# Moving stores and transposing transfers from the sync queue to GpSimd's queue in a Macaron S4D layer

## The chip, the core and the metric

The kernel runs on one core of one Trainium2 chip. The metric is the device time in microseconds of one execution; the figure for a kernel is the median of several runs. The names in the profile are: PE is TensorE's matmul queue and PEld its weight loads, DVE is VectorE, ACT is ScalarE, POOL is GpSimd, SP is SyncE (which here only issues transfers). A name with a q behind it, such as SPq, is an engine's own instruction queue: the time in which it issues a transfer or waits to do so.

## The reference

A Macaron layer on x of shape 4 x 1024 x 256: half a feed-forward network, then a state-space (S4D) convolution along the sequence, then half of the same feed-forward network again. Each part normalises its input and adds its result to it.

```
x = x + 0.5 * ffn(layernorm(x))
x = x + s4d(layernorm(x))
x = x + 0.5 * ffn(layernorm(x))

def ffn(x):
    h = silu((x @ w1.T) * s1) * ((x @ w2.T) * s2)     # 256 -> 1024
    h = gelu((h @ h1.T) * s3)                          # 1024 -> 1024
    h = gelu((h @ h2.T) * s4)                          # 1024 -> 1024
    return (h @ w3.T) * s5                             # 1024 -> 256

def s4d(x):                    # per channel, along the 1024 positions
    K = 2 * Re(sum_n C_n * exp(dtA_n * t))
    y = irfft(rfft(x, 2048) * rfft(K, 2048))[:1024]
    return gelu(y) @ W.T + b
```

The gelu is the exact one. The weights w1, w2, h1, h2 and w3 are ternary (-1, 0, 1).

## The kernel before

The tokens are cut into 16 feed-forward blocks of 512: eight "f" blocks take x to the intermediate x1, eight "g" blocks take x2 to the output. One batch element is two blocks. Between an f pair and a g pair lies the convolution of that batch element, `mix(b)`, which takes x1 to x2. All intermediates (x1, x2, the spectrum `k_hat`, and a scratch array `moved`) lie in DRAM.

A block's matmuls run in four stages. Layer 1 is 16 groups of four matmuls (`pa`, `pb`). Layers 2 and 3 are eight groups of 16 matmuls each, 128x512 outputs. The output product `po` has 64 matmuls of 128x256. Activations come in two parts, a rounded value and the rest that rounding left (`low_part`, L257), so each weight tile is used with both. ScalarE does the activation and the rounding, VectorE the rest. After `po`, VectorE scales the result (L375), GpSimd adds the residual `xr` (L383) and the sum is stored (L384).

The convolution is work for every engine, in small steps, and these steps are woven into the feed-forward blocks. `tick()` is called after each output of layers 2 and 3 (15 times a block) and advances the generator `aside` by one step: first the convolution's kernel (`pk`, L595 to L625), then its spectrum (matrices `m_k`, results stored in `k_hat`), then the four mixes. A mix loads half a batch element (`xm`, L173), normalises it, multiplies it by the transform's matrices (`m_m`, loaded at L653, product `pf_m` at L664), multiplies by the spectrum (L759 to L761), transforms back (`pi`, matrices `mi`), and applies W (`pw`), whose result `yw` gets its residual on GpSimd (L868) and is stored (L869).

From the fifth block on, every third tick also advances `weight_checks`: 44 steps, each of which loads a piece of a weight (`given`, L418) and counts where it differs from its rounded copy. At the end the counts are reduced (`total`, L433), a matmul adds the partitions (`p_bad`, L435) and the result goes to `bad`. After the layer a register loads `bad`; if it isn't 0, the layer is run again at full precision.

`ahead()` is called after each output of layer 3 and advances `prepare` for the next block: load its x (`load_x`, L188, four transfers of 128 KB), normalise (L234 to L244), and `squares` (L276). The latter is a transpose by way of DRAM: VectorE transposes 32x32 squares (`sq`, L282), eight transfers of 64 KB put them at their places in `moved` (L286), two transfers of 256 KB bring `moved` back as `xf` (L292). When layer 3 is through, `parted` (L301, L257) makes the two parts `xt` that the next block's layer 1 reads.

Before the change all of these transfers after the start are issued by SP, in one order. The program is written in one order of statements; a list scheduler of the framework reorders within each engine, with its own estimates of times, and places the waits. Each engine runs its instructions in order, so an instruction that waits holds those behind it. What lies behind what on SP is set by this order. Three pools matter: the tag `xb` (x, xm, x_g before normalisation) has three buffers, `half` has 19[...].

In the first block GpSimd issues the weight loads and the first x loads.

Of the kernel before, what the change touches and what calls it, by code (L numbers as in the profile page):

```python
# [94 lines left out]
def macaron_layers(  # L95
# [23 lines left out]
    nc = tc.nc  # L119
# [39 lines left out]
    x2 = dram.tile([B, L, D], F32, name="x2")  # L159

    moved = dram.tile([DC, P, JT, P], F32, name="moved")
    k_hat = dram.tile([2 + len(PAIRS), 2, P, 2, D], F32, name="k_hat")
# [4 lines left out]
    def positions(t, b, j, n=2):  # L167
        return t[b].rearrange("(p j) d -> p j d", j=J)[:, j : j + n, :]
# [8 lines left out]
    def tokens(t, blk, a=0, n=JT):  # L177
        b, g = divmod(blk, J // JT)
        rows_of = t[b, g * TB : (g + 1) * TB, :]
        return rows_of.rearrange("(q a) d -> q a d", a=JT)[:, a : a + n, :]  # L180
# [11 lines left out]
        return w.rearrange("(k p) o -> p k o", p=P)  # L192


    weights_from = nc.gpsimd if split else nc.sync

    x_first = work.tile([P, JT, D], F32, tag="xb", name="x_f0", bufs=3)
# [78 lines left out]
    def squares(xn, name):  # L276


        out = []
        for k in range(DC):  # L280
            sq = half(f"sq_{name}_{k}", P // SQ, JT, SQ)
            nc.vector.transpose(  # L282
                sq, xn[:, :, k * P : (k + 1) * P].rearrange("p j (c r) -> p c j r", r=SQ)
            )
            for a in range(JT):
                nc.sync.dma_start(  # L286
                    moved[k].rearrange("(c r) a q -> a r c q", r=SQ)[a],
                    sq[a * SQ : (a + 1) * SQ].rearrange("r c j s -> r c (j s)"),
                )
        for k in range(DC):  # L290
            t = half(f"xf_{name}_{k}")
            nc.sync.dma_start(t, moved[k].rearrange("d a q -> d (a q)"))  # L292
            out.append(t)
        return out

# [23 lines left out]
    def ffn(xt, src, dst, blk, name, tick, ahead, final):  # L319

        ha = []
        for m in range(KH):
            pa, pb = bank(f"pa_{name}_{m}"), bank(f"pb_{name}_{m}")
            linear(pa, w1_sb, m, xt)
            linear(pb, w2_sb, m, xt)
            g = half(f"g_{name}_{m}")
            t = ring(f"ha_{name}_{m}", parts, TB, dtype=wide)
            nc.scalar.activation(g, pa, AF.Silu, scale=sc_sb[:, 0, m : m + 1])  # L330
            stt(g if split else t[:, 0, :], pb, sc_sb[:, 1, m : m + 1], g, ALU.mult, ALU.mult)
            if split:
                nc.scalar.copy(t[:, 0, :], g)  # L333
                low_part(t, g)
            ha.append(t)
        for layer, w in ((2, h1_sb), (3, h2_sb)):
            hb = []
            for m in range(KH):
                ps = bank(f"p{layer}_{name}_{m}")
                linear(ps, w, m, ha)  # L340
                t = ring(f"h{layer}_{name}_{m}", parts, TB, dtype=wide)
                g = half(f"g{layer}_{name}_{m}") if split else t[:, 0, :]
                nc.scalar.activation(g, ps, AF.Gelu, scale=sc_sb[:, layer, m : m + 1])  # L343
                if split:
                    nc.scalar.copy(t[:, 0, :], g)  # L345
                    low_part(t, g)
                hb.append(t)
                if layer == 3:
                    ahead()
                if m < KH - 1:  # L350
                    tick()
            ha = hb
        ahead(last=True)
        tick()
        rest = []
        for i in range(0, JT, 2):
            xr = half(f"xr_{name}_{i}", 2, D)
            nc.sync.dma_start(xr, tokens(src, blk, i, 2))
            rest.append(xr)

        def result(ps, i, n):

            for e in range(n):
                for k in range(KH):
                    for part in range(parts):
                        nc.tensor.matmul(  # L366
                            ps[:, e * D : (e + 1) * D],
                            ha[k][:, part, (i + e) * P : (i + e + 1) * P],
                            w3_sb[:, k, :],
                            start=(k == 0 and part == 0),  # L370
                            stop=(k == KH - 1 and part == parts - 1),
                        )

        def finish(ps, y, xr, i, n, add_on):
            stt(  # L375
                y,
                ps.rearrange("p (e d) -> p e d", e=n),
                0.5,
                w3s_sb[:, None, :].to_broadcast([P, n, D]),
                ALU.mult,  # L380
                ALU.mult,
            )
            add_on.tensor_tensor(y, xr, y, ALU.add)  # L383
            nc.sync.dma_start(tokens(dst, blk, i, n), y)  # L384

        for i in range(0, JT, 2):
            y = half(f"y_{name}_{i}", 2, D)
            if final and i + 2 == JT:
                for e in range(2):
                    ps = bank(f"po_{name}_{i + e}")  # L390
                    result(ps, i + e, 1)
                    finish(
                        ps[:, 0:D],
                        y[:, e : e + 1, :],
                        rest[i // 2][:, e : e + 1, :],
                        i + e,
                        1,
                        nc.vector,
                    )
            else:  # L400
                ps = bank(f"po_{name}_{i}")
                result(ps, i, 2)
                finish(ps, y, rest[i // 2], i, 2, nc.gpsimd)

    def weight_checks():

        todo = []
        for src, held in ((w1, w1_sb), (w2, w2_sb), (h1, h1_sb), (h2, h2_sb), (w3, w3_sb)):
            n_k, width = held.shape[1], held.shape[2]
            by = max(1, 512 // width)  # L410
            for k in range(0, n_k, by):
                for c in range(0, width, 512):
                    cols = slice(c, min(c + 512, width))
                    todo.append((rows(src)[:, k : k + by, cols], held[:, k : k + by, cols]))
        assert len(todo) == N_CHECKS
        for n, (src, held) in enumerate(todo):
            given = half(f"given_{n}", *held.shape[1:])
            nc.sync.dma_start(given, src)  # L418
            stt(
                given,  # L420
                given,
                0.0,
                held.bitcast(F32),
                ALU.add,
                ALU.not_equal,
                accum_out=miss[:, n : n + 1],
            )
            yield

        total = small.tile([P, 1], F32, name="total")  # L430
        ones = small.tile([P, 1], F32, name="ones")
        nc.vector.memset(ones, 1.0)
        nc.vector.tensor_reduce(total, miss[:, 0:N_CHECKS], axis=mybir.AxisListType.X, op=ALU.add)  # L433
        ps = psum.tile([1, 1], F32, tag="ps", name="p_bad")
        nc.tensor.matmul(ps, total, ones, start=True, stop=True)  # L435
        nc.vector.tensor_copy(bad, ps)
# [276 lines left out]
    def kernel_spectrum():  # L713

        def rows_of(j):
            return taps[j // 2][:, j % 2].rearrange("p h d -> p (h d)")

        got = None
        for got in spectrum(rows_of, "k", over=NB // J):
            yield  # L720
        minus = half("k_minus", 2, D)
        for n, m in enumerate((0, 4)):
            t = got[m]
            nc.scalar.mul(minus[:, n, :], t[:, 1, :], -1.0)
            for e in range(2):
                nc.sync.dma_start(k_hat[n, 0, :, e], t[:, 0, :])
            nc.sync.dma_start(k_hat[n, 1, :, 0], minus[:, n, :])
            nc.sync.dma_start(k_hat[n, 1, :, 1], t[:, 1, :])
            yield
        for n, (a, b) in enumerate(PAIRS):  # L730
            n += 2
            minus = half(f"k_minus_{n}", 2, D)
            t, o = got[a, b], got[b, a]
            nc.scalar.mul(minus[:, 0, :], o[:, 1, :], -1.0)
            nc.sync.dma_start(k_hat[n, 0, :, 0], t[:, 0, :])
            nc.sync.dma_start(k_hat[n, 0, :, 1], o[:, 0, :])
            nc.sync.dma_start(k_hat[n, 1, :, 0], minus[:, 0, :])
            nc.sync.dma_start(k_hat[n, 1, :, 1], t[:, 1, :])
            yield

    def mix(b):
# [23 lines left out]
        r, i = factors(0)  # L765
# [6 lines left out]
        for n, (p, q) in enumerate(PAIRS):  # L772
            r, i = following
# [72 lines left out]
        for j in range(0, J, 2):  # L846
# [19 lines left out]
                ALU.add,  # L866
            )
            nc.gpsimd.tensor_tensor(y, xr, y, ALU.add)  # L868
            nc.sync.dma_start(positions(x2, b, j), y)  # L869
        yield  # L870


# [147 lines left out]
```

## Time and profile before

| | us |
|---|---|
| median of 3 runs | 1464.32 (1463.37 to 1466.54) |
| the profiled execution | 1462.53 |
| its span, first to last instruction | 1460.8 |
| DVE busy | 839.0 (57%) |
| ACT busy | 682.4 (47%) |
| mean granted TensorE clock | 0.987 of full |

Device time of the profiled execution is 1.7 us above its span; the profile's rows refer to the span.

The queues, from the page: transfers, MB, and the share that their packets took of the 16 DMA engines' time.

```profile
q1 hardware_dynamic: 64800, 85.79, 18.7%
q0 software_dynamic: 5168, 13.96, 2.9%
```

The hardware queue carries what SP and ScalarE issue, the software queue what GpSimd issues. The longest stays of SP's queue before an instruction (total us, times, longest us):

```profile
SPq L286 <- DVE sq_f L282: 229.2, 7, 69.8
SPq L384 <- POOL y_g L383: 146.0, 15, 62.9
SPq L286 <- DVE sq_g L282: 129.9, 8, 57.5
SPq L384 <- POOL y_f L383: 93.4, 16, 17.1
SPq L869 <- POOL yw L868: 76.9, 16, 16.1
```

Most of this is time in which SP has nothing else that it could usefully do; the row alone doesn't tell how much. Times from issue to landing of the transfers that the change concerns, and of loads behind them (medians, us): moved 1.7, xf 2.8 (g) and 3.4 (f), stores of y 2.0, stores of yw 3.0, k_hat 1.7 to 1.8; m_m 4.5, m_k 4.3, xm 4.1, x_g 3.3. Of transfers that GpSimd issues: x_f 7.5, w_sb 4.3 (256 KB) to 21.1 (1 MB), all in the start, where 361 GB/s are moved in the first fortieth of the span against a mean of 69.

Reading the timeline: start, duration, engine, line, operation, output and inputs, how many, and in brackets how long the engine had been idle and what ended it. Durations of an SPq row are those of issuing, not of the transfer. For the DMA rows of POOL the same holds.

### The profile page before, as it was taken

To read this page: it belongs to the slowest core of one execution; us is meant where nothing else is said; L and a number is where in the kernel's file an instruction comes from. 1 tells how busy PE (TensorE), PEld (TensorE's weight loads), DVE (VectorE), ACT (ScalarE), POOL (GpSimd) and SP (SyncE) were. 2 spreads that over 40 slices of the span, in tenths; PEclk is the share of its full clock that TensorE was granted. 3 is DMA by queue.
4 is the path that set the end of the run, shared out by engine and by line. 5 is a ranking of instruction groups with operands and counts; after the bars stand their busy time and mean duration, and the time that the engine had idled before them with its cause. 6 is when DMAs were issued, how large, how long until landed. Compare 5 with 4: busy or idle time off the path is not lost.

```text
span 1460.8 us, 18295 instructions
## 1 busy us (share of the span) xinstructions
PE 1418.2 (97%) x6972; PEld 1197.8 (82%) x6972; DVE 839.0 (57%) x1614; ACT 682.4 (47%) x1037; POOL 87.6 (6%) x91
## 2 busy tenths in 40 slices
PE   9999999998999999999999998999979989999997
PEld 7878888887888888888788887888868878888886
DVE  6886657743735687453877534857436757351421
ACT  5875468644435444343353433534245334353442
POOL 4010000100000000010000010000000000100000
PEclk9999999999999999999999999999989999999999
DMA  9120201102123140240332123231240320210200
GB/s 361 40 71 0 59 15 35 39 8 80 55 76 101 44 159 17 85 130 15 109 94 72 59 79 102 67 99 45 71 145 16 94 65 32 93 49 1 65 8 18
DMA packets 70210, 101.27 MB, mean 69 GB/s; under 512 B 7952, under 2 KB 34832, under 8 KB 70112
## 3 DMA queue, kind: packets, MB, share of 16 engines
q1 hardware_dynamic: 64800, 85.79, 18.7%
q0 software_dynamic: 5168, 13.96, 2.9%
q8 instruction: 56, 0.92, 0.3%
q14 instruction: 42, 0.34, 0.1%
q10 hardware_dynamic: 144, 0.26, 0.1%
HBM read 76.91 MB, written 23.07 MB: 68 GB/s over the span
## 4 chain that ended last, share of the span: by engine, by line
PE 89%; DVE 3%; DMA 3%; ACT 2%; SPq 1%; issue 1%; POOL 0%; DVEq 0%; POOLq 0%
PE p_g L311 30%; PE p_f L311 27%; PE po_g L366 4%; PE pa_f L311 4%; PE pa_g L311 4%; PE pb_f L311 4%; PE pb_g L311 4%; PE po_f L366 3%; PE pf_m L664 2%; PE pi L834 2%; PE pw L854 2%; PE pk L595 1%; SPq L286 1%; DMA m_m<-in_cosm_dram 1%; PE pf_k L664 0%
## 5 line engine op out<-in xcount | busy, mean ns | idle before, releaser
L311 PE MATMUL p_f<-h_f,h_sb 128*128 128x512 f32 x1024 | 239.3, 392 | 0.0
L311 PE MATMUL p_g<-h_g,h_sb 128*128 128x512 f32 x1024 | 238.4, 393 | 0.0
L311 PE MATMUL p_f<-ha_f,h_sb 128*128 128x512 f32 x1024 | 237.2, 391 | 0.0
L311 PE MATMUL p_g<-ha_g,h_sb 128*128 128x512 f32 x1024 | 235.0, 390 | 0.0
L311 PEld LDWEIGHTS p_g<-h_g,h_sb 128*128 128x128 f32 x1024 | 194.0, 189 | 40.7
L311 PEld LDWEIGHTS p_g<-ha_g,h_sb 128*128 128x128 f32 x1024 | 192.1, 188 | 39.7
L311 PEld LDWEIGHTS p_f<-h_f,h_sb 128*128 128x128 f32 x1024 | 191.8, 188 | 39.9
L311 PEld LDWEIGHTS p_f<-ha_f,h_sb 128*128 128x128 f32 x1024 | 191.6, 188 | 40.1 <-ACT ha_f L333 0.2
L257 DVE TENSOR_TENSOR h_g<-g_g,h_g 128x512 fp32r<-128x512 f32 x128 | 88.2, 690 | 230.4 <-ACT h_g L345 230.4
L343 ACT ACTIVATE g_g<-p_g,sc_sb 128x512 f32<-128x512 f32 x128 | 88.3, 690 | 282.2 <-PE p_g L311 274.4
L257 DVE TENSOR_TENSOR h_f<-g_f,h_f 128x512 fp32r<-128x512 f32 x128 | 87.8, 690 | 189.7 <-ACT h_f L345 189.3
L343 ACT ACTIVATE g_f<-p_f,sc_sb 128x512 f32<-128x512 f32 x128 | 88.1, 689 | 216.6 <-PE p_f L311 198.4
L345 ACT CAST h_g<-g_g 128x512 fp32r<-128x512 f32 x128 | 79.1, 620 | 3.7
L345 ACT CAST h_f<-g_f 128x512 fp32r<-128x512 f32 x128 | 78.5, 618 | 2.9
L330 ACT ACTIVATE g_g<-pa_g,sc_sb 128x512 f32<-128x512 f32 x64 | 43.7, 689 | 76.7 <-PE pa_g L311 73.4
L311 PE MATMUL pa_g<-xt_g,w_sb 128*128 128x512 f32 x256 | 69.8, 391 | 2.6 <-DVE xt_g L301 2.6
L311 PE MATMUL pa_f<-xt_f,w_sb 128*128 128x512 f32 x256 | 70.1, 392 | 2.0 <-DVE xt_f L301 1.3
L366 PE MATMUL po_f<-w_sb,h_f 128*128 128x256 f32 x512 | 67.3, 291 | 4.3 <-DVE h_f L257 3.0
L366 PEld LDWEIGHTS po_f<-w_sb,h_f 128*128 128x128 f32 x512 | 65.7, 198 | 6.4 <-DVE h_f L257 3.9
L311 PE MATMUL pb_f<-xt_f,w_sb 128*128 128x512 f32 x256 | 69.2, 390 | 0.0
L311 PE MATMUL pb_g<-xt_g,w_sb 128*128 128x512 f32 x256 | 69.0, 390 | 0.0
L366 PE MATMUL po_g<-w_sb,h_g 128*128 128x256 f32 x512 | 66.4, 291 | 0.1
(231 smaller groups left out, 1632.7 us busy)
## 6 DMA issues: line engine op xcount, KB each, us to landing
h_sb<-in_h_dram POOLq DMA_DIRECT2D x8, 1024.0 KB, 12.9
given<-in_h_dram SPq DMA_DIRECT2D x32, 256.0 KB, 3.3
kr<-k_hat SPq DMA_DIRECT2D x20, 256.0 KB, 2.7
ki<-k_hat SPq DMA_DIRECT2D x20, 256.0 KB, 3.1
xr_f<-in_x_dram SPq DMA_DIRECT2D x16, 256.0 KB, 3.6
x<-y_f SPq DMA_DIRECT2D x16, 256.0 KB, 2.0
xm<-x SPq DMA_DIRECT2D x8, 512.0 KB, 4.1
m_m<-in_cosm_dram SPq DMA_DIRECT2D x16, 256.0 KB, 4.5
```

Source lines behind the costliest of these rows:

```text
L257: return tt(t[:, 1, :], src, t[:, 0, :].bitcast(F32), ALU.subtract)
L286: nc.sync.dma_start(moved[k].rearrange("(c r) a q -> a r c q", r=SQ)[a], sq[a * SQ : (a + 1) * SQ].rearrange("r c j s -> r c (j s)"),)
L311: nc.tensor.matmul(ps, w[:, k, m * P : (m + 1) * P], acts[k][:, part, :], start=(k == 0 and part == 0), stop=(k == n - 1 and part == parts ...
L330: nc.scalar.activation(g, pa, AF.Silu, scale=sc_sb[:, 0, m : m + 1])
L343: nc.scalar.activation(g, ps, AF.Gelu, scale=sc_sb[:, layer, m : m + 1])
L345: nc.scalar.copy(t[:, 0, :], g)
L366: nc.tensor.matmul(ps[:, e * D : (e + 1) * D], ha[k][:, part, (i + e) * P : (i + e + 1) * P], w3_sb[:, k, :], start=(k == 0 and part == 0) ...
L595: nc.tensor.matmul(pk[0:NA, at + i, :, :].rearrange("p h b -> p (h b)"), a[:, i].rearrange("p a b -> p (a b)"), qd[d1 // per_tile][:, at + ...
L664: nc.tensor.matmul(ps[e][:, part, :], m[:, e, part, :], rows_of(q + JQ * e), start=True, stop=True)
L834: nc.tensor.matmul(banks[dc][e][:, q * P : (q + 1) * P], vs[q + JQ * e][:, part, dc * P : (dc + 1) * P], m[:, e, part, :], start=(part == ...
L854: nc.tensor.matmul(ps[:, e * D : (e + 1) * D], yts[dc][j // JQ][:, (j % JQ + e) * P : (j % JQ + e + 1) * P], wt_sb[:, dc, :], start=(dc == 0),
```

## The change

All stores to x1, x2 and `k_hat`, the stores of the output but for the last block's three, and the squares' ten transfers per block are issued on GpSimd's queue. SP keeps the loads. In counts: 120 transfers to `moved`, 30 loads of `xf`, 30 token stores, 20 stores to `k_hat`, 16 stores to x2, so 216 in all. On GpSimd they stand in one order with its additions. The reduction of the weight checks' counts and the product `p_bad` are put into two steps of `weight_checks` in place of one; between them lie three ticks.

```diff
+    stores = nc.gpsimd
...
             for a in range(JT):
-                nc.sync.dma_start(
+                stores.dma_start(
                     moved[k].rearrange("(c r) a q -> a r c q", r=SQ)[a],
                     sq[a * SQ : (a + 1) * SQ].rearrange("r c j s -> r c (j s)"),
                 )
         for k in range(DC):
             t = half(f"xf_{name}_{k}")
-            nc.sync.dma_start(t, moved[k].rearrange("d a q -> d (a q)"))
+            stores.dma_start(t, moved[k].rearrange("d a q -> d (a q)"))
...
             add_on.tensor_tensor(y, xr, y, ALU.add)
-            nc.sync.dma_start(tokens(dst, blk, i, n), y)
+            (nc.sync if final else stores).dma_start(tokens(dst, blk, i, n), y)
...
         nc.vector.tensor_reduce(total, miss[:, 0:N_CHECKS], axis=mybir.AxisListType.X, op=ALU.add)
+        yield
         ps = psum.tile([1, 1], F32, tag="ps", name="p_bad")
...
             for e in range(2):
-                nc.sync.dma_start(k_hat[n, 0, :, e], t[:, 0, :])
+                stores.dma_start(k_hat[n, 0, :, e], t[:, 0, :])
...
             nc.gpsimd.tensor_tensor(y, xr, y, ALU.add)
-            nc.sync.dma_start(positions(x2, b, j), y)
+            stores.dma_start(positions(x2, b, j), y)
```

The other six stores to `k_hat` are changed in the same way.

More of the change, by code (lines that the diff above doesn't have):

```diff
@@ L725, in kernel_spectrum @@
             for e in range(2):
-                nc.sync.dma_start(k_hat[n, 0, :, e], t[:, 0, :])
-            nc.sync.dma_start(k_hat[n, 1, :, 0], minus[:, n, :])
-            nc.sync.dma_start(k_hat[n, 1, :, 1], t[:, 1, :])
+                stores.dma_start(k_hat[n, 0, :, e], t[:, 0, :])
+            stores.dma_start(k_hat[n, 1, :, 0], minus[:, n, :])
+            stores.dma_start(k_hat[n, 1, :, 1], t[:, 1, :])
             yield
@@ L734, in kernel_spectrum @@
             nc.scalar.mul(minus[:, 0, :], o[:, 1, :], -1.0)
[L735 to L738, printed above, removed]
+            stores.dma_start(k_hat[n, 0, :, 0], t[:, 0, :])
+            stores.dma_start(k_hat[n, 0, :, 1], o[:, 0, :])
+            stores.dma_start(k_hat[n, 1, :, 0], minus[:, 0, :])
+            stores.dma_start(k_hat[n, 1, :, 1], t[:, 1, :])
             yield
```

## The prediction

> **What bounds the kernel now.** I read the page's busy table first, then TensorE's waits, then the timeline around each long wait, then the chain that ended last for what follows each wait.
>
> ```profile
> PE 1418.2 (97%) x6972; PEld 1197.8 (82%) x6972; DVE 839.0 (57%) x1614; ACT 682.4 (47%) x1037; POOL 87.6 (6%) x91
> ```
>
> TensorE is the bound: 1460.8 span less 1418.2 busy leaves 42.6 us. The change takes no matmul away, so only idle time and slow matmuls can be gained. The waits of TensorE say where the idle time is (total us, times, longest):
>
> ```profile
> PE pf_m L664 <- DMA m_m<-in_cosm_dram: 13.2, 2, 9.0
> PE p_bad L435 <- DVE total L433: 4.8, 1, 4.8
> PE pf_k L664 <- DMA m_k<-in_cosm_dram: 4.7, 1, 4.7
> PE po_f L366 <- DVE h_f L257: 3.0, 4, 1.1
> PE pa_g L311 <- DVE xt_g L301: 2.6, 1, 2.6
> ```
>
> The first three rows are four gaps: 4.2, 9.0, 4.8 and 4.7, together 22.7 us. Three of them wait for a matrix load. The timeline shows why those loads were late; gap 1, at 344.7:
>
> ```profile
> 337.70 1.30 DVE L282 STREAM_TRANSPOSE sq_f<-x_f 128x512 f32<-128x512 f32 x2
> 338.43 3.72 SPq L286 DMA_DIRECT2D moved<-sq_f  x8
> 342.33 0.34 SPq L292 DMA_DIRECT2D xf_f<-moved  x1
> 342.71 0.43 SPq L173 DMA_DIRECT2D xm<-x  x1
> 343.48 0.32 SPq L292 DMA_DIRECT2D xf_f<-moved  x1
> 343.84 3.67 SPq L653 DMA_DIRECT2D m_k<-in_cosm_dram  x6
> 349.33 3.46 PE L664 MATMUL pf_k<-taps,m_k 128*128 128x256 f32 x8 [4.66 <-DMA m_k<-in_cosm_dram]
> ```
>
> The sync queue (SPq) sits on the squares' transfers from 338.43 to 343.80, and the matrix loads come behind. Gap 3, at 1076.05, has the same form:
>
> ```profile
> 1073.82 1.30 DVE L282 STREAM_TRANSPOSE sq_g<-x_g 128x512 f32<-128x512 f32 x2
> 1074.56 3.70 SPq L286 DMA_DIRECT2D moved<-sq_g  x8
> 1078.88 0.42 SPq L188 DMA_DIRECT2D x_g<-x  x1
> 1080.07 0.38 SPq L653 DMA_DIRECT2D m_m<-in_cosm_dram  x1
> 1085.06 3.75 PE L664 MATMUL pf_m<-xm,m_m 128*128 128x256 f32 x8 [9.01 <-DMA m_m<-in_cosm_dram]
> ```
>
> Gap 2 (at 888.9) is between them: its matrix load is issued at 888.12 and lands at 892.9. Gap 4 is the flag's product, stuck between layer 3 and the output product:
>
> ```profile
> 1186.78 0.19 DVE L433 TENSOR_REDUCE total<-miss 128x1 f32<-128x44 f32 x1
> 1187.12 0.19 PE L435 MATMUL p_bad<-ones,total 128*1 128x1 f32 x2 [4.83 <-DVE total L433]
> ```
>
> The chain shows that a gap costs more than its wait: matmuls just after it run slower.
>
> ```profile
> 1187.31 10.27 PE po_g L366 x64
> ```
>
> An undisturbed po product takes 7.67, so 2.6 more. By the same comparison gap 1 carries +2.0 (eight pf_k in 3.46 where the next group's piece in the chain has 1.73, then 0.3), gap 2 +3.2, gap 3 +2.8. The ceiling is 22.7 + 10.6 = about 33 us.
>
> [...]eight moved and two xf issues, with the wait for moved between them, held the queue for 5.4 us before gap 1, and the 16 engines are lightly used (hardware queue 18.7%). [...]
>
> **The change part by part.**
> *Off the sync queue:* 120 moved, 30 xf, 30 token stores, 20 k_hat stores and 16 x2 stores, 216 in all; three stores of the last block stay. SP issues them at 0.32 to 0.47 us. What SP does now is reach its next load sooner. But the next load in its order is itself bound: the xb buffers number three, so the load of xm or x_g can't start before the transposes L282 have read the buffer it overwrites, and matrix loads stand behind that load.
>
> - Gap 1: the xm load stands free at 339.0 (transposes' end), takes 0.43, and the six m_k follow at 0.61 each. The pair needed is issued by about 340.2 in place of 344.4 (the second of six); with the median landing of 4.3 us it lands at 344.5, wanted at 344.67. Gain: 4.2 of the wait and most of the slow matmuls; bounds 3 to 6.6, I take 5.5.
> - Gap 2: the four x_g loads issue at 883.3 to 885.1 and the matrix load at 885.3 in place of 888.12; landing 4.5 to 4.8 later is 889.8 to 890.1, against 888.9 wanted. The wait falls from 4.2 to about 1.2, plus some 2 of the slow start; bounds 2 to 7.4, taken 5.
> - Gap 3: the changed kernel's order puts the normalisation of xm (L244, four of 0.35 us) before the transposes, so these end near 1077.1, not 1075.1. x_g's four issues then end at 1079.0 and the matrix load goes then, 1.1 earlier than 1080.07. The gap shrinks from 9.0 to about 7.7, and its slow start stays; bounds -1 (the transposes later still) to 4, taken 1.3.
> - Gap 4: in the changed order p_bad stands between two layer-2 outputs of the next block; total is then long done. The flag is read after it by SP's register load, ahead of loads needed only at 1244.7. Gain 4.8 + 2.6, less two small matmuls of 0.19; bounds 4 to 7.4, taken 6.6.
>
> Sum of gains 18.4.
>
> *Onto gpsimd:* the nearest row is gpsimd's own loads[...]:
>
> ```profile
> L188 POOL DMA_DIRECT2D x_f<-in_x_dram x12 | 6.6, 558 | 11.1 <-DMA h_sb<-in_h_dram 7.4 <-DVE k_a L443 3.0 <-DMA wt_sb<-in_wt_dram 0.7
> ```
>
> 216 x 0.558 = 121 us, POOL from 87.6 to about 208, 14% busy; no bound. Its additions (1.3 to 1.4 us) and the stores behind them feed loads a block or more later. Two costs can reach TensorE.
>
> First, the chain transposes, moved, xf, L301. Before: 3.7 issue + 1.75 landing + 0.34 + about 3.1 = 8.9 us. After: 8 x 0.558 = 4.5, + 2.1 + 0.56 + 3.5 = 10.7[...]. So xf lands about 1.8 us later. From xf's landing to L301 the trace of before leaves between 5 and 17 us in 13 of 15 blocks, 0 in the block ending at 1283 and 2 in that at 1363; there a late L301 holds h_7's low part, which the last of the 64 output matmuls need (3.4 us of cover). I take +1.5 for both; bounds 0 and 4.
>
> Second, VectorE's order. Freed loads arrive earlier, and the changed order puts their statistics (L234) ahead of h_5 or h_6 in most blocks; VectorE waits there for the load, then h_7 can be late for po. The waits of po_f in before are 1.1 at most. I take 0.4 in 14 blocks, +5.5; bounds 0 and 1.1 each, 15. Vector operations that reuse sq's buffers wait for moved to be read (one 1.0 us wait at 1175.7 in before): +1, bounds 0 and 3.
>
> Net: -18.4 + 1.5 + 5.5 + 1 = -10.4. Profiled execution 1462.5 - 10.4 = 1452.1; the median shown lies 1.8 above the profiled one, so 1453.9, about 1454.
>
> **Rivals.**
> 1. *All four gaps go.* The freed queue leads all loads enough and nothing is late: -33 with costs near 0, 1431 to 1440. For it: 5.4 us of queue time against waits of 4.2 to 9.0. Against: the wait for the transposes stays ahead of gap 3. Chance 0.10.
> 2. *Given back.* Only gap 4 and about half of gaps 1 and 2 are gained (12), and VectorE's waits for earlier statistics plus the xf delay take the same at their upper ends (1.1 x 8 + 3): 1462 to 1467. Chance 0.14.
> 3. *Slower: gpsimd's transfers land late.* In before its x_f loads have a median of 7.5 us to landing, though beside weight traffic. With 7.5 twice in the chain: 4.5 + 7.5 + 0.56 + 7.5 = 20, or 11 us later than before. Taking from each of the 15 blocks its slack and 3.4 of cover leaves 7.6 and 5.6 in the two tight blocks and 1.6 to 2.6 in five more, 24 in all: -10.4 - 1.5 + 24 = +12, 1476. It decides from about 9 us of extra delay, where these losses reach the net gain. For it: every block passes through this chain and gpsimd waits in order, moved before xf. Against: away from startup the DMA engines are mostly free, and same-sized gpsimd loads of w_sb, also amid weights, took 4.3. Chance 0.20, with smaller losses of this sort joined to stalls on VectorE.
>
> That gpsimd's issue doesn't help at all is excluded by the built order of instructions: of 621 on SP, 362 remain.
>
> **How the numbers follow.** My forecast, partial gain, has 0.56, and its own range is 1446 to 1461. This measurement can tell about 0.2%, or 2.9 us. Faster: 0.56 + 0.10 = 0.66; same 0.14; slower 0.20. The range for 8 in 10 cuts half of rival 1 below and about half of rival 3 above: 1440 to 1472.
>
> **What would show it.** Right: no p_bad row among the waits; the pf_k wait under 1; the pf_m waits 13.2 to about 9, one of them still 7 to 8 near 1084; POOL about 205 us; moved near 2.1 and xf near 3.5 to landing; small new po waits. Wrong: xf landing over 5, or pa rows waiting for xt_g L301 in many blocks (rival 3); po rows of over 8 us in sum waiting for h L257 (rival 2); no pf_m wait (rival 1). If gpsimd's issues took over 1 us each, my first cost would be too small by 4 us a block.

## The result, and the profile after

The changed kernel takes 1448.48 us (median of 4 runs, 1448.20 to 1450.36), against 1464.25 for the kernel before in the same comparison. The ratio is 0.9893, with a 95% interval of 0.9876 to 0.9910. The profiled execution took 1448.43 us, 14.1 less than the profiled one of before; its span is 1446.6, so the two spans differ by 14.2. These 14.2 us are what the traces can account for.

The busy table of the changed kernel (its lines are two to three higher than those of before):

```profile
PE 1413.5 (98%) x6972; PEld 1194.2 (83%) x6972; DVE 842.5 (58%) x1614; ACT 675.6 (47%) x1031; POOL 205.6 (14%) x307
```

The number of matmuls is the same, yet PE's busy time is 4.7 us less: there are fewer slow matmuls behind gaps. POOL's 205.6 stands against the estimate of 208. The waits of PE (total us, times, longest us):

```profile
PE pf_m L667 <- DVE h_g L259: 9.5, 1, 9.5
PE po_f L368 <- DVE h_f L259: 5.9, 4, 2.5
PE po_f L368 <- ACT h_f L347: 2.8, 1, 2.8
PE warm L926 <- POOL ident masks.py:199: 2.6, 1, 2.6
PE pa_g L313 <- DVE xt_g L303: 1.9, 1, 1.9
PE pf_m L667 <- DMA m_m<-in_cosm_dram: 1.8, 1, 1.8
```

The rows of p_bad and pf_k are gone, and one pf_m wait went from 4.2 to 1.8. The other stays at 9.5, and the waits of po have grown. Gap 1 in the timeline of the changed kernel:

```profile
340.80 1.30 DVE L284 STREAM_TRANSPOSE sq_f<-x_f 128x512 f32<-128x512 f32 x2
341.80 4.37 POOL L288 DMA_DIRECT2D moved<-sq_f  x8 [61.17 <-DVE sq_f L284]
342.13 0.33 SPq L173 DMA_DIRECT2D xm<-x  x1
...
342.51 3.77 SPq L656 DMA_DIRECT2D m_k<-in_cosm_dram  x6
```

From the start of the transposes to the first of these m_k issues it was 6.14 us (337.70 to 343.84); now it is 1.71. Gap 3 in the changed kernel, by contrast:

```profile
1069.78 1.30 DVE L284 STREAM_TRANSPOSE sq_g<-x_g 128x512 f32<-128x512 f32 x2
...
1071.11 1.81 SPq L188 DMA_DIRECT2D x_g<-x  x4
...
1073.03 0.37 SPq L656 DMA_DIRECT2D m_m<-in_cosm_dram  x1
...
1079.24 3.75 PE L667 MATMUL pf_m<-xm,m_m 128*128 128x256 f32 x8 [9.46 <-DVE h_g L259]
```

The squares no longer stand on SP, but x_g's four issues do, and they can't start before the transposes have ended (1071.08). The matrix load is issued at 1073.03 and takes 6.1 us to land (the shortest of the four m_m in this stretch), 1079.1: this is what ended the wait, though the row names VectorE, whose h_g came at about the same time. In the trace of run 5, the same kernel once more, the row names the load (12.1 us for both pf_m waits), and there as here the product starts 0.14 us after the first m_m has landed.

Where the 14.2 us come from: the time from the first layer-2 product of a block to that of the next one, in both traces (blocks numbered from 0). At these points TensorE has done the same number of matmuls in both kernels, in block 13 but for the two of p_bad. At the first pa of a block it has not: there the order of pa and the last po products differs between the kernels, by 34 matmuls in block 2 and 36 in block 3.

| from layer 2 of block | before | after | difference | in it |
|---|---|---|---|---|
| 0 to 2 | 175.48 | 172.72 | -2.76 | po and pa waits at 86 to 90 |
| 2 to 3 | 82.26 | 87.98 | +5.72 | po waits at 261 to 263 |
| 3 to 4 | 103.99 | 97.78 | -6.21 | gap 1 |
| 4 to 7 | 263.10 | 262.48 | -0.62 | |
| 7 to 8 | 92.64 | 95.79 | +3.15 | po wait at 715.8 |
| 8 to 9 | 80.58 | 80.24 | -0.34 | |
| 9 to 10 | 108.68 | 103.33 | -5.35 | gap 2 |
| 10 to 12 | 191.56 | 191.69 | +0.13 | gap 3 |
| 12 to 13 | 89.58 | 81.97 | -7.61 | gap 4 |
| 13 to the end | 248.81 | 248.36 | -0.45 | |

With 0.14 at the start the sum is -14.20. The trace of run 5 gives the same picture: no row differs by more than 0.4 from these. The place of the largest loss in the kernel before:

```profile
263.10 4.33 PE L366 MATMUL po_f<-w_sb,h_f 128*128 128x256 f32 x34 [0.46 <-DVE h_f L257]
```

and in the changed kernel:

```profile
247.07 0.33 SPq L173 DMA_DIRECT2D xm<-x  x1
251.19 1.40 DVE L236 BATCH_NORM_STATS2 stats_m<-xm 128x6 f32<-128x256 f32 x4 [3.53 <-DMA xm<-x]
...
261.49 1.22 PE L368 MATMUL po_f<-w_sb,h_f 128*128 128x256 f32 x4 [2.47 <-DVE h_f L259]
```

The freed load of xm comes earlier, VectorE's order has its statistics ahead of h_5 to h_7, VectorE stands 3.53 us for the load, and po waits for h. At 715.8 the statistics of xm stand ahead of h in the same way, but VectorE waits only 0.66 us for the load. At the end of block 0 the earlier load is of x_f, and it helped: before, waits of 0.98, 1.27 and 1.32 follow each other there; after, one of 2.82 is left.

The transfers themselves, median us to landing, in the changed kernel:

```profile
moved<-sq_g POOLq DMA_DIRECT2D x64, 64.0 KB, 2.0
xf_g<-moved POOLq DMA_DIRECT2D x16, 256.0 KB, 3.1
...
moved<-sq_f POOLq DMA_DIRECT2D x56, 64.0 KB, 3.4
xf_f<-moved POOLq DMA_DIRECT2D x14, 256.0 KB, 3.3
```

From the first issue of moved to the landing of the second xf the mean over the 15 blocks went from 8.9 us to 11.4. The longest, 15.7, is in the block of gap 3.

### The profile page after: what moved, and what is told of

Its sections match the earlier page's. It is cut to its first block, busy times and chain, and to the rows that moved or that the text cites. A ratio compares the mean times of both kernels' runs of the same rounds, so it can differ in the third digit from the quotient of the medians.

```text
span 1446.6 us, 18389 instructions
## 1 busy us (share of the span) xinstructions
PE 1413.5 (98%) x6972; PEld 1194.2 (83%) x6972; DVE 842.5 (58%) x1614; ACT 675.6 (47%) x1031; POOL 205.6 (14%) x307
## 2 busy tenths in 40 slices
DMA packets 49986, 101.27 MB, mean 70 GB/s; under 512 B 7952, under 2 KB 16912, under 8 KB 49888
## 4 chain that ended last, share of the span: by engine, by line
PE 88%; DVE 4%; ACT 3%; DMA 2%; issue 1%; POOL 1%; SPq 0%; DVEq 0%; POOLq 0%
PE p_g L313 30%; PE p_f L313 27%; PE po_g L368 4%; PE pa_f L313 4%; PE pa_g L313 4%; PE pb_f L313 4%; PE pb_g L313 4%; PE po_f L368 4%; PE pi L837 2%; PE pf_m L667 2%; PE pw L857 1%; PE pk L598 1%; DMA xm<-x 1%; ACT g_f L345 1%; ACT L345 1%
## 5 line engine op out<-in xcount | busy, mean ns | idle before, releaser
L288 POOL DMA_DIRECT2D moved<-sq_g x64 | 35.1, 556 | 350.8 <-DVE sq_g L284 348.9
L288 POOL DMA_DIRECT2D moved<-sq_f x56 | 30.5, 553 | 318.2 <-DVE sq_f L284 318.2
## 6 DMA issues: line engine op xcount, KB each, us to landing
h_sb<-in_h_dram POOLq DMA_DIRECT2D x8, 1024.0 KB, 11.7
```

The source lines that it names most:

```text
L288: stores.dma_start(moved[k].rearrange("(c r) a q -> a r c q", r=SQ)[a], sq[a * SQ : (a + 1) * SQ].rearrange("r c j s -> r c (j s)"),)
```

## The experiments

All ratios are to runs of the kernel before on the same chip, with 95% intervals. Different sets ran on different chips.

### 1. The flag alone

```diff
 # kernel before
         nc.vector.tensor_reduce(total, miss[:, 0:N_CHECKS], axis=mybir.AxisListType.X, op=ALU.add)
+        yield
```

> The kernel before with only the flag's product one step later. My theory: gap 4 goes whole, its wait of 4.8 us and the slow output product behind it (2.6 us), so 7 to 8 us below before (about 1457), no p_bad row among the waits, and the pf_k and pf_m waits stay at 4.7 and 13.2. Rival, that a product between two outputs of the next block breaks TensorE's stream elsewhere or the check's order shifts: 0 to 4 us gained, with new waits of PE.

Measured: 1455.93 us against 1462.44, ratio 0.9959 (0.9942 to 0.9975), so 6.5 us. The p_bad row is gone and block 12, which holds gap 4, went from 89.58 to 81.97: 7.6 us, as expected. But pf_m's waits rose from 13.2 to 16.2: gap 3 grew to 11.95, in a trace in which VectorE waited 1.63 us for a weight piece (given) ahead of the transposes, and these came 2.1 us later against the product that waits. So gap 4 is worth 7.6, and the length of gap 3 depends on small shifts in VectorE's order.

### 2, 3 and 4. All moves without the flag; the squares alone; the stores alone

```diff
 # run 2: the changed kernel without the added yield
 # run 3: the kernel before, and in squares()
-                nc.sync.dma_start(
+                nc.gpsimd.dma_start(
                     moved[k].rearrange("(c r) a q -> a r c q", r=SQ)[a],
...
-            nc.sync.dma_start(t, moved[k].rearrange("d a q -> d (a q)"))
+            nc.gpsimd.dma_start(t, moved[k].rearrange("d a q -> d (a q)"))
 # run 4: run 2, with these two on nc.sync
```

> All 216 transfers on gpsimd, the flag's product where it was before. My theory: the two parts add up, so this is about 8 us faster than before (1464.3 to about 1456), the p_bad wait stays near 4.8, pf_k's wait is gone, pf_m's near 11. Rival, that the parts depend on each other: more than 3 us away from 1456.

> Only the squares' transfers (moved and xf, 150 of the 216) on gpsimd; all stores stay on the sync queue, the flag stays. Theory A, the squares are what held the sync queue ahead of the matrices: all of the gain of the moves, about 1456, pf_k and the first pf_m wait gone or under 2. Theory B, stores that wait on the sync queue for gpsimd's additions hold the loads: within 2 us of before, 1464.

> Only the 66 stores (x1, out, x2, k_hat) on gpsimd, the squares stay on the sync queue, the flag stays. Theory A: within 2 us of before, 1464, the waits of pf_k (4.7) and pf_m (13.2) as in before. Theory B: most of the gain, about 1456.

| run | us | ratio to before |
|---|---|---|
| all moves | 1457.24 | 0.9968 (0.9955 to 0.9980) |
| squares alone | 1457.78 | 0.9970 (0.9962 to 0.9978) |
| stores alone | 1461.64 | 0.9996 (0.9988 to 1.0005) |

Theory A holds for the times: the squares alone gain what all moves gain, 5 us, and the stores alone gain nothing. The stays of SP's queue at the stores, 146, 93 and 77 us in the table of before, held no load whose lateness showed in the time. In the trace of run 4 pf_k's wait is 5.3 and pf_m's are 16.1, not the 4.7 and 13.2 that were expected: gap 3 is 11.7 long, much as in run 1. With the squares alone pf_k's wait is 0.4 and the first pf_m wait 1.4, and the po waits are those of the changed kernel (2.9 at 261, 2.5 at 715.6): the cost comes with the squares' move too.

That runs 2 and 3 take the same time hides two differences. In run 3 gap 3 is 7.0 long where it is 8.9 in run 2, and its matmuls end 3.2 us sooner; but what comes after the last matmul is longer (us, from the traces):

| | last matmul ends | span | between |
|---|---|---|---|
| before | 1452.6 | 1460.8 | 8.1 |
| changed | 1439.2 | 1446.6 | 7.3 |
| run 2 | 1446.3 | 1453.8 | 7.5 |
| run 3 | 1443.1 | 1454.6 | 11.5 |
| run 4 | 1454.7 | 1461.1 | 6.4 |
| run 6 | 1438.5 | 1449.1 | 10.6 |
| run 8 | 1434.2 | 1445.6 | 11.4 |

In this time the last results are stored and the engines close the program. In runs 3, 6 and 8 GpSimd's closing DRAIN instruction takes 7.6, 6.9 and 7.6 us, against 4.3 in the changed kernel and run 2. It differs between kernels whose GpSimd queues carry different transfers; why was not tested.

### 5. The changed kernel again

> The changed kernel once more, on the chip of the next three runs, as their measure. From the first comparison: 0.989 of before, about 15 us less; from the sum of its two parts as measured alone (6.5 and 5.2): 0.992, about 11.7 less. Which of the two it is tells whether the parts add up.

Measured: 1449.68 against 1463.84, ratio 0.9910 (0.9886 to 0.9935). Both 0.989 and the 0.9927 that the two parts alone give (0.0041 and 0.0032) lie within the interval, so this run doesn't decide. Nor do the spans of the single traces: flag -5.1, moves -7.0, both -14.2 and in this run's trace -13.3. The 1.2 to 2.1 us between are less than the spread of single executions (1458.9 to 1466.4 for the kernel before on the chip of runs 1 to 4). Gap 3, which grew by 2.9 in run 1, is a place where the parts can differ in sum; whether they add up stays open.

### 6. x_g on gpsimd's queue

```diff
 # the changed kernel; prepare()
-            xb = load_x(x2, blk, f"x_{name}")
+            xb = load_x(x2, blk, f"x_{name}", nc.gpsimd)
```

> The changed kernel, and the loads of x_g (four per g block) on gpsimd's queue too, so that no matrix load stands behind a load that waits for the transposes. Theory A, gap 3 (9.5 us and about 2.5 of slow matmuls) is head-of-line waiting behind x_g on the sync queue: gap 3 goes, and the rest of gap 2 (1.8): 10 to 14 us below the changed kernel. Theory B, the matrix's own buffer or the crowd of transfers behind the transposes limits it: within 3 us of the changed kernel, pf_m's wait still 7 or more. Against A would also be new waits of PE for xt_g, because x_g comes later.

Measured: 1451.35, ratio 0.9919 (0.9895 to 0.9942): no gain over the changed kernel (0.9910). The place of gap 3 in its timeline:

```profile
1047.96 0.33 SPq L656 DMA_DIRECT2D m_m<-in_cosm_dram  x1
...
1069.33 2.25 PE L667 MATMUL pf_m<-xm,m_m 128*128 128x256 f32 x8
...
1072.42 0.70 DVE L284 STREAM_TRANSPOSE sq_g<-x_g 128x512 f32<-128x512 f32 x1
...
1077.11 0.56 POOL L188 DMA_DIRECT2D x_g<-x  x1
...
1079.62 0.57 POOL L294 DMA_DIRECT2D xf_g<-moved  x1 [1.95 <-DMA moved<-sq_g]
1080.17 1.64 POOL L188 DMA_DIRECT2D x_g<-x  x3
...
1086.27 1.41 DVE L236 BATCH_NORM_STATS2 stats_g<-x_g 128x6 f32<-128x256 f32 x4 [11.97 <-DMA x_g<-x]
...
1091.34 0.58 PE L368 MATMUL po_g<-w_sb,h_g 128*128 128x256 f32 x1 [7.59 <-ACT h_g L347]
```

The matrix is issued 21 us ahead of its product, and pf_m waits no more: theory A had the cause of gap 3 right. Its time was wrong. The late x_g now holds VectorE, which stands 11.97 us at its statistics with h_g behind them, and po waits 7.59 in place of pf_m's 9.46. Only part of this is the wait for the buffer. The transposes ended at 1073.1, and three of the four x_g loads were issued 7 us after that, at 1080.17: on GpSimd's queue they stood behind the squares' transfers and the wait for moved. In the changed kernel the four issues began right at the transposes' end, and VectorE stood 5.77 us. So x_g was held by its buffer and then by its new queue. From layer 2 of block 10 to that of 12 it is 191.87, the price of before. The rest of gap 2 did go: from layer 2 of block 9 to that of 10 it is 101.27 in place of 103.33. This gain shows in no time, since the end of the run is 3.3 us longer (the table above).

### 7 and 8. xm on gpsimd's queue, and both

```diff
 # run 7: the changed kernel, load_half(); run 8: with run 6's edit too
-        nc.sync.dma_start(xb, positions(t, b, g * JT, JT))
+        nc.gpsimd.dma_start(xb, positions(t, b, g * JT, JT))
```

> The changed kernel, and the loads of xm on gpsimd's queue, where they stand behind the squares' transfers, about as late as in the kernel before. Theory A, what the change gives back is VectorE's order: the statistics of an early xm stand ahead of h_5 to h_7, and po waits (2.5 at 261 and 2.5 at 716): these two waits fall to 0.5 as in before, 3 to 5 us below the changed kernel. Theory B, it is the later xf: the waits stay, the time is within 1.5 us of the changed kernel's or above.

> Both of the last two edits. If the head-of-line wait and VectorE's order are separate causes, the gains add up: 13 to 18 us below the changed kernel, about 1433 where before is 1464. If gpsimd's queue itself now holds what is needed (x_g, xm, squares and additions in one order), less than the better one alone, with waits of PE for xt_g or pf_m.

Run 7: 1450.29, ratio 0.9905 (0.9876 to 0.9934). The po wait at 716 fell from 2.5 to 0.5, as theory A had it; that at 261 stayed (2.2), for a new reason, and the time is the changed kernel's. The gain at 716 (3.1 us from layer 2 of block 7 to that of 8) and one of 2.3 between blocks 2 and 3 were paid back: a new po wait of 2.14 at 532 cost 3.2, and gap 3 grew from 9.5 to 12.2, 3.3 more from block 10 to 12. The new reason at 261:

```profile
254.47 0.54 POOL L294 DMA_DIRECT2D xf_f<-moved  x1 [1.85 <-PE p_f L313]
255.01 1.01 POOL L580 MEMSET qd<- 128x512 f32 x2
...
255.59 1.72 DVE L584 TENSOR_TENSOR qd<-k_b,a_b 64x256 f32<-64x256 f32 x4 [6.11 <-POOL qd L580]
```

GpSimd's clearing of qd stood behind the second xf, which was issued 0.54 us after the last moved had landed (at 253.93; the row names PE); VectorE waited 6.11 us for it. Run 8: 1448.99, ratio 0.9908 (0.9883 to 0.9934). The gains don't add up to what was hoped: pf_m's long wait is gone, and po waits 6.5 at 1087.6 for h_g. Something was gained all the same: the last matmul ends at 1434.2, 5 us sooner than in the changed kernel, and 4 us of it go to the longer end.

### 9, 10 and 11. A fourth buffer of xb

```diff
 # run 9: the changed kernel; run 11: the kernel of run 1
-        xb = work.tile([P, JT, D], F32, tag="xb", name=name, bufs=3)
+        xb = work.tile([P, JT, D], F32, tag="xb", name=name, bufs=4)
-        return work.tile([P, *(shape or (512,))], dtype, tag="half", name=name, bufs=19)
+        return work.tile([P, *(shape or (512,))], dtype, tag="half", name=name, bufs=17)
 # the other two tiles of xb likewise; run 10: the changed kernel with half's edit alone
```

> The changed kernel with a fourth buffer under the tag xb, paid for with two buffers of half (19 to 17). Now x_g and xm need not wait for the transposes, so neither the matrix loads on the sync queue nor the statistics on VectorE have a late load before them. Theory A, the third buffer is what makes gap 3 last (whatever queue stands behind it): no pf_m wait and no po wait near 1080 to 1091, 8 to 13 us below the changed kernel. Theory B, the transfers or VectorE's order limit it: gap 3 or its like stays, within 3 us.

> Control for the run with the fourth buffer: the changed kernel with 17 buffers of half and three of xb. If 17 are enough, within 2 us of the changed kernel; if not, some us slower, which then is to be added to the gain of the fourth buffer.

> The kernel before with the flag's product later, and with four buffers of xb and 17 of half, all transfers on the sync queue. Theory A, loads wait for two things, the squares on the queue and the buffer: with the buffer alone gap 3 shrinks and gaps 1 and 2 may go too, since the loads may pass ahead of the squares; 1445 to 1452. Theory B, the squares on the queue are what counts and the buffer is nothing without the move: about 1457, as with the flag alone.

| run | us | ratio to before |
|---|---|---|
| 9, four buffers, moves | 1441.14 | 0.9844 (0.9812 to 0.9875) |
| 10, three buffers, 17 of half | 1453.10 | 0.9921 (0.9896 to 0.9946) |
| 11, four buffers, flag, no moves | 1448.01 | 0.9906 (0.9875 to 0.9937) |

Theory A holds in run 9 in the main: no pf_m wait is left, and from layer 2 of block 10 to that of 12 it is 183.57 in place of 191.69. A po wait of 2.08 is left at 1086.6, where A wanted none: VectorE stands 1.79 us for the second xf there, with h_g behind it. Against its control, run 10, the buffer is worth 12 us. The control itself lies 0.1 to 0.3% (2 to 4 us) above the changed kernel's two ratios (0.9893 and 0.9910), with intervals that overlap. Run 11 is inside what A expected (1445 to 1452), but its gaps are 3.5, 4.5 and 7.9 us, against 4.8, 4.3 and 11.9 in run 1: gap 2 did not shrink, and the three give 5.2 of the 9.5 us by which run 11's span is shorter. In gap 3 its matrix load still stands behind the squares and xf on SP. The flag and a buffer thus come to about the changed kernel's ratio without a transfer moved; moves and buffer together gave more than either.

The longest waits that are left in run 9 are that at 1086.6, one of po at 89 (3.12) and those of po and pa near 266 (3.50, 0.49, 1.49), of the kind seen in run 7.

### 12. The two orders at 266

```diff
 # run 9's kernel, with run 7's edit, and in kernel_steps()
-                    nc.gpsimd.memset(t, 0.0)
+                    nc.vector.memset(t, 0.0)
```

> The kernel with four xb buffers (1441), and two edits against what the move gives back at 266: xm's loads on gpsimd's queue behind the squares, so that their statistics stand behind h_5 on VectorE, and the clearing of qd on VectorE in place of gpsimd, where it stood behind xf (VectorE waited 6.1 us for it when xm alone was moved). Theory A, these two orders are what po waits for at 266 (3.5 + 0.5, then 1.5 for xt_f): these waits fall under 1 in sum, 3 to 5 us less, about 1437. Theory B, the later xf or the total work of VectorE before h_7 sets it: the waits at 266 stay above 3 in sum and the time is within 2 us of 1441 or above.

Measured: 1435.15 against 1464.51, ratio 0.9801 (0.9780 to 0.9821), the fastest of all. Its longest waits of PE:

```profile
PE po_f L368 <- ACT h_f L347: 3.7, 2, 3.1
PE pa_g L313 <- DVE xt_g L303: 2.6, 1, 2.6
PE warm L926 <- POOL ident masks.py:199: 2.6, 1, 2.6
PE po_f L368 <- DVE h_f L259: 1.8, 3, 1.0
PE pf_k L667 <- DMA m_k<-in_cosm_dram: 1.4, 1, 1.4
```

Near 263 a po wait of 0.97 and a pa wait of 0.62 remain, 1.6 in sum where run 9 had 5.5. That is not quite the "under 1" that A asked for, but far below B's 3, and blocks 2 and 3 take 182.96 against 190.14. The order of the statistics, of the memset or of both was the cause there; the two edits were not separated.

## Why the prediction was right

The forecast was partial gain, 1454 with a range of 1440 to 1472; the time is 1448.5. By its steps:

- *Gap 1.* Taken at -5.5, with the load landing just in time. Its wait (4.66) is gone, and the time from layer 2 of block 3 to that of block 4 is 6.21 less. The trace shows the mechanism that was named: SP goes from xm straight to m_k.
- *Gap 2.* Taken at -5 with a rest of 1.2: its stretch lost 5.35, and 1.8 is left.
- *Gap 3.* Taken at -1.3, from 9.0 to about 7.7: it is 9.46, and its stretch +0.13; pf_m's waits sum to 11.3, where about 9 was named as the sign. This step was wrong. The changed order of VectorE and x_g's four issues ahead of the matrix are as read; what was missed is the landing, 6.1 us where before had 4.85, with x_g and moved in flight beside it. That the matrix stands behind x_g, and x_g behind its buffer, which the prediction had named as the reason for taking little, is shown by run 6 (the matrix freed from x_g) and run 9 (x_g freed from the buffer): in both pf_m's wait is gone.
- *Gap 4.* Taken at -6.6: 7.61 here, and 7.6 in run 1.
- *The moved transfers.* 216 issues at 0.558: the moved ones took 553 to 556 ns, POOL is busy for 205.6. moved lands in 2.0 for g (2.1 expected) but 3.4 for f; xf in 3.1 and 3.3 (3.5 expected). The 2.1 and 3.5 were the author's estimate: before's trace has none of these transfers on GpSimd's queue. In three blocks all eight moved land in 1.9 to 2.1; in the others some take longer, up to 6.7 in gap 3's block, where x_g and m_m are in flight. Whether loads in flight are the cause was not tested. The chain grew by 2.5 us, not 1.8. As a median, rival 3's landings of 7.5 did not come about. The tight blocks at 1283 and 1363 lost nothing that shows: from layer 2 of block 13 to the end it is 0.45 less, where +1.5 was taken.
- *VectorE's order.* Taken at 0.4 in 14 blocks, +5.5. Measured, it is nothing in most blocks, 5.72 at 261 (2.8 of added waits, the rest matmuls slowed after them: PE is busy 84.74 us for the stretch's 402, against 81.80 in before) and 3.15 at 716, 8.9 in sum. Run 7 shows the cause for the one at 716, and run 12, with the memset, for that at 261. At 88 the same kind of change gained 2.7; no run was made to separate it. Of before's waits of po_f the prediction read the row of VectorE (1.1 at most); there is also one of 1.27 for ScalarE, in this place.

The gains by the four gaps sum to 19.0 (18.4 taken), the two losses to 8.9; block 0 gave 2.7 and the quiet stretches 1.3: -14.2. The forecast's net of -10.4 was thus short by 3.8: 0.6 from the gaps, 2.5 from the terms for xf and for the reuse of buffers, which didn't show, 2.7 from block 0 and 1.3 from the quiet stretches, less 3.4 by which VectorE's losses were larger than taken. So the gaps were understood, all but gap 3. That the sum came near is in part luck: VectorE's loss was right in kind, but larger and in two places where it was spread over 14 blocks, and a gain at block 0 that was not forecast made up for most of the difference. The medians differ by 15.8, 1.6 more than the spans; the second comparison (0.9910) gives 14.2.

The prediction also said of the 216 transfers that SP reaches its loads sooner, without saying which of them matter. Run 4 shows that 66 of them, the stores, are worth nothing that can be measured in the time.

## What to carry to other kernels

A queue's long stays before a store don't tell what they cost (316 us in three rows of before, and nothing gained in run 4, 0.9996): ask which late load stands behind which instruction, and move that instruction alone. When a load waits for a buffer, moving it to another queue frees what stood behind it, but not the load; on the new queue it can also stand behind something else (run 6: pf_m's 9.46 us went, po waits 7.59). One more buffer removes the wait, once the queue is free of the squares (run 9: no pf_m wait left, 12 us less than run 10); with the flag's later product and no transfer moved it gave about as much as the whole change (run 11, 0.9906 against 0.9893 and 0.9910). Work that becomes ready early, such as the statistics of a freed load, can stand ahead of what the bound engine needs (VectorE stood 3.53 us for xm, with the h that po waited 2.47 us for behind it), and so can a transfer ahead of a small memset (VectorE waited 6.11 us for qd in run 7). Look at the end of the trace too: what comes after the last matmul took from 6.4 to 11.5 us here, and hid gains of 3 to 4 us.

## What the runs showed of the hardware

In these traces the length of TensorE's idle time alone doesn't tell how slow the matmuls behind it are. From the chain of waits of the changed kernel, behind gap 2 (1.79 us) and gap 3 (9.46 us), with an undisturbed group last:

```profile
889.75 1.97 PE pf_m L667 x8
...
1079.24 3.75 PE pf_m L667 x8
1082.99 4.09 PE p_g L313 x16
1087.08 1.73 PE pf_m L667 x8
```

After 1.79 us of idle eight matmuls took 1.97 (0.24 more than 1.73); after 9.46 they took 3.75, 2.2 times as long as undisturbed, and the next 16 p_g took 4.09, where the 16 behind the last row took 3.64. Between these lengths both are seen. Run 11 after 3.46 us, and the changed kernel before and after 2.52 us:

```profile
349.60 1.97 PE L665 MATMUL pf_k<-taps,m_k 128*128 128x256 f32 x8 [3.46 <-DMA m_k<-in_cosm_dram]
...
710.37 2.91 PE L368 MATMUL po_f<-w_sb,h_f 128*128 128x256 f32 x22
715.80 2.07 PE L368 MATMUL po_f<-w_sb,h_f 128*128 128x256 f32 x8 [2.52 <-DVE h_f L259]
```

Eight pf_k after 3.46 us took 1.97, the same as the eight pf_m after 1.79. But po takes 0.26 us a matmul after 2.52 us of idle, where it took 0.13. Behind gaps of 4.18 and 9.01 us in before, 4.49 in run 11, 9.24 in run 10, 9.46 in the changed kernel and 11.95 in run 1, eight pf_m took 3.75; behind the 4.66 in before eight pf_k took 3.46. Gap 2, cut from 4.18 to 1.79, lost its tail: the eight pf_m and the 16 p_g behind it took 8.60 us in before and 5.64 in the changed kernel, where undisturbed ones take 5.37. With hardly a gap left, run 12 needs 1408.9 us of PE for the same 6972 matmuls (1418.2 before), at a mean granted clock of 0.996 (0.987).

The queues of the changed kernel, from the page:

```profile
q1 hardware_dynamic: 33696, 55.36, 12.3%
q0 software_dynamic: 16048, 44.38, 9.1%
```

Against before, the same 30.4 MB left the hardware queue with 31104 packets and 6.4% of the engines' time, and went over the software queue in 10880 packets and 6.2%. So the move cut the packets to about a third, and the time that they take hardly changed.

The issues of the 216 transfers took 540 to 574 ns on GpSimd's queue in the changed kernel (means by kind of transfer), against 558 for the x_f loads that GpSimd issues in before; VectorE was busy for 58% of the span. Why moved lands later for f (3.4 us) than for g (2.0) stays open.
